# Layers 0 and 1 of a four-layer hybrid network: the convolution reads PSUM by image, the output projection runs among the steps of the scan, and the row update of layer 1 moves into layer 2

## The chip, the cores and the metric

One core of a Trainium2 chip runs the whole network once. The metric is the device time of that one launch in microseconds (us); less is better. Five engines work from queues of their own, each in order: TensorE (PE, matrix products and transposes into PSUM), VectorE (DVE), ScalarE (ACT), GpSimd (POOL), and SyncE (SP), which issues transfers. ACT and POOL issue transfers too.

## The reference

The input is four images of 256 channels by 1024 positions, in float32. What is computed, cut to what this change touches:

```python
# layer 0
u = layernorm(x)                                  # over the 256 channels of a position
zxbcdt = u @ in_w.T                               # z 256, xBC 512, dt 4
dt = softplus(dt + dt_bias)
xBC = silu(causal_depthwise_conv(xBC, conv_w, 4 taps) + conv_b)
for t in range(1024):                             # state: 4 heads of 64 x 128
    state = state * exp(-dt * exp(A_log)) + (dt * x_t) B_t;  y_t = state @ C_t
y = rms_normalise((y + Dp * x) * silu(z)) * rms_w
out = y @ out_w.T
att = sigmoid(relu(mean_over_positions(out) @ se1_w.T + se1_b) @ se2_w.T + se2_b)
x = x + out * att                                 # one att per image
# layer 1: theta, phi, g are products of x with one column each
y = theta * (sum_over_positions(phi * g) / 1024)  # per image
x = x + batchnorm(w_w * y + w_b) * bn_gamma + bn_beta   # statistics over all images
# layer 2: attention per image, then 8 experts, 2 for each row; layer 3: linear attention, then an LSTM of 1024 steps
```

## The kernel before

Positions lie on the 128 partitions: an image is 8 row tiles of 128 positions, the whole input is 32 row tiles. `s.rows` holds all 32 of them (256 floats a partition each) from layer 0 to the end of layer 2's attention. Float32 products appear in the profile as two PE instructions each, transposes as one.

**Projection** (`_project`, L215). Eight blocks of 512 positions. `load` fetches a block of x, turns it into rows (L241, L244) with the three columns of layer 1 beside it (L245), and normalises it (L133, L134 on DVE, L146, L147 on POOL, L153 on DVE). `turn` turns the normalised rows back (L162, L257), `project` makes z and dt (L270, L273, L274) and the four 128-channel chunks of xBC (L278), which ACT copies from PSUM to SBUF behind three columns of zeros (L281). After each second block `convolve` makes the four taps of a chunk: one on ACT (L288), three on DVE (L293), then silu on ACT (L296). PSUM has 2 slots for `p_x`, 4 for `p_w` and 2 for `p_z`.

**Decays** (`_decays`, L311). After the last block, once for all 32 tiles: softplus by Exp and Ln, then three products and Exp.

**Scan** (`_scan`, L356). Per tile of 128 positions: five products and transposes (L370, L371), the mask of decays (L381 on ACT, L383, L385, L386), the product inside the tile (L392), the state's share and the state's update (L401 to L409), then the gate (L412) and its squares (L414).

**Output** (`_out`, L417). Per image: 1/rms of 8 tiles (L426, L427 on POOL), diagonal matrices (L434) with which PE turns and scales the rows (L438, L442), their sum, the two small layers of the attention (L451 to L467), the weight times that attention (L469), six products with accumulation for the three columns of layer 1 (L473), and 8 products (L481) added to the rows (L484, L485). It is written after the scan of the next image; for the last image nothing follows it but layer 1.

**Layer 1** (`_layer1`, L488). A chain of small operations over all images (L505 to L549), `bn_beta` added to the rows on POOL (L552, 8 instructions) and 32 row updates on DVE (L554).

**Layer 2** (`_layer2_attention`, L575) loads its weights (L123), makes the product of the query and key weights (L602, L608), and then runs `front(b)` per image (`norm`, `turn`, `query`, `value`); the front of image b + 1 runs beside the scores of image b. After it `_lstm_constants` (L1281) loads and scales the LSTM's weights (L1286, L1289, L1290), and the plan of the experts follows (`_plan`, L957).

Outside blocks marked `manual_schedule` a planner orders the instructions of each engine: what is written first has the higher priority, but what is ready by its own estimates may go ahead. Tiles take their memory from pools; a tile waits until its slot is free.

Of the kernel before, what the change touches and what calls it, by code (L numbers as in the profile page):

```python
# [71 lines left out]
NW = {"w_l0": 260 + 512 + 256 + 64, "w_l2": 768 + 8, "w_l3": 768, "w_u": 768, "w_v": 768}  # L72
# [92 lines left out]
def _layer0_and_1(s):  # L165

    nc, tc = s.nc, s.tc
    off = DCONV - 1  # L170
    with ExitStack() as ctx:
        keep = ctx.enter_context(tc.tile_pool(name="l0_keep", bufs=1))
        w = keep.tile([P, C, NW["w_l0"]], F32, name="w_l0")
        nc.scalar.dma_start(w, s.d["w_l0"].rearrange("(k p) n -> p k n", p=P))
        se2 = keep.tile([NSE, D], F32, name="se2")
        nc.scalar.dma_start(se2, s.d["w_se2"])
        wide = keep.tile([P, 5, D], F32, name="wide")
        nc.scalar.dma_start(
            wide.rearrange("p i d -> p (i d)"), s.d["wide"].to_broadcast([P, 5 * D])
        )  # L180
        v = SimpleNamespace(
            w_zdt=w[:, :, :ZDT], w_xbc=w[:, :, ZDT : ZDT + 512], w_out=w[:, :, 772:1028],
            w_se1=w[:, :, 1028:1092], se2=se2, se2_b=wide[:, 0, :], beta=wide[:, 1, :],
            three=wide[:, 2:, :],
# [3 lines left out]
            xbc=[keep.tile([P, NXBC, off + L], F32, name=f"xbc{b}") for b in range(B)],  # L188
            zs=[keep.tile([P, TPI, D], F32, name=f"zs{b}") for b in range(B)],
            dtr=keep.tile([P, NT, NH], F32, name="dtr"),  # L190
            ss=keep.tile([P, NT], F32, name="ss"),
        )
        for x in v.xbc:
            nc.gpsimd.memset(x[:, :, :off], 0.0)
        for k in range(C):
            nc.vector.tensor_scalar_mul(
                v.w_out[:, k, :], v.w_out[:, k, :], s.col["rms_w"][:, k : k + 1]
            )
        _project(s, v)
        v.dt, v.decay, v.total, v.tail = _decays(s, keep, v.dtr)  # L200
        with ExitStack() as body:
            pools = SimpleNamespace(
                scan=body.enter_context(tc.tile_pool(name="ssm", bufs=2)),
                out=body.enter_context(tc.tile_pool(name="out", bufs=2)),
                ps=body.enter_context(tc.tile_pool(name="ssm_ps", bufs=2, space=PSUM)),
            )
            for b in range(B):
                _scan(s, v, pools, b)
                if b > 0:
                    _out(s, v, pools, b - 1)  # L210
            _out(s, v, pools, B - 1)
        _layer1(s, v)


def _project(s, v):  # L215
# [4 lines left out]
    with ExitStack() as ctx:  # L220
        one = ctx.enter_context(tc.tile_pool(name="proj_one", bufs=1))
        pool = ctx.enter_context(tc.tile_pool(name="proj", bufs=2))
        ps = ctx.enter_context(tc.tile_pool(name="proj_ps", bufs=3, space=PSUM))

        turner = one.tile([P, C, 3 + P], F32, name="turner")
        for k in range(C):
            nc.vector.tensor_copy(turner[:, k, 3:], s.ident)
            for j, name in enumerate(("theta_w", "phi_w", "g_w")):
                nc.vector.tensor_copy(turner[:, k, j : j + 1], s.col[name][:, k : k + 1])
        held = {}  # L230

        def load(i):
# [4 lines left out]
            for j in range(TPB):  # L237
                n = i * TPB + j
                p = ps.tile([P, C, 3 + P], F32, name="p_x", bufs=2)
# [6 lines left out]
            at = slice(i * TPB, (i + 1) * TPB)  # L246
            held[i] = _moments(s, pool, lambda j: s.rows[:, i * TPB + j, :], TPB)
            un = pool.tile([P, TPB, D], F32, name="un")
            _normalise(s, pool, un, s.rows[:, at, :], held[i])
            held[i] = un  # L250

        def turn(i):
            u = pool.tile([P, C, W], F32, name="u")
            for k in range(C):
                p = ps.tile([P, W], F32, name="p_w", bufs=4)
                _turn(s, p.rearrange("p (j t) -> p j t", t=P), held[i], k)
                nc.scalar.activation(  # L257
                    u[:, k, :], p, AF.Identity,
                    bias=s.col["norm_b"][:, k : k + 1], scale=s.col["norm_g"][:, k : k + 1],
                )  # L260
            held[i] = u

        def project(i):
            u = held.pop(i)
            b, t0 = divmod(i * W, L)
            for j in range(TPB):
                n = t0 // P + j
                p = ps.tile([P, ZDT], F32, name="p_z", bufs=2)
                for k in range(C):
                    nc.tensor.matmul(  # L270
                        p, u[:, k, bass.ts(j, P)], v.w_zdt[:, k, :], start=k == 0, stop=k == C - 1
                    )
                nc.scalar.activation(v.zs[b][:, n, :], p[:, :D], AF.Silu)  # L273
                nc.vector.tensor_add(v.dtr[:, b * TPI + n, :], p[:, D:], s.row["dt_bias"])  # L274
            for m in range(NXBC):
                p = ps.tile([P, W], F32, name="p_w", bufs=4)
                for k in range(C):
                    nc.tensor.matmul(  # L278
                        p, v.w_xbc[:, k, bass.ts(m, P)], u[:, k, :], start=k == 0, stop=k == C - 1
                    )  # L280
                nc.scalar.copy(v.xbc[b][:, m, off + t0 : off + t0 + W], p)  # L281

        def convolve(b):
            for m in range(NXBC):
                x = v.xbc[b][:, m, :]
                acc = pool.tile([P, L], F32, name="acc")
                tap = s.col["conv_w"][:, m * DCONV : (m + 1) * DCONV]
                nc.scalar.activation(  # L288
                    acc, x[:, off:], AF.Identity,
                    bias=s.col["conv_b"][:, m : m + 1], scale=tap[:, off:],  # L290
                )
                for j in range(off):
                    nc.vector.scalar_tensor_tensor(  # L293
# [281 lines left out]
def _layer2_attention(s):  # L575
# [10 lines left out]
    with ExitStack() as ctx:  # L586
# [222 lines left out]
        with tc.manual_schedule(engines=IN_ORDER):  # L809
# [13 lines left out]
            f.last()  # L823


def _layer2_experts(s):

# [838 lines left out]
```

## Time and profile before

| What | us |
|---|---|
| Median of 3 runs (3480.51 to 3481.63) | 3481.63 |
| The profiled execution, its own time | 3482.43 |
| Its span (first to last instruction) | 3480.7 |
| PE busy over the span | 3121.1 |
| DVE busy over the span | 1841.5 |
| ACT busy over the span | 1091.2 |
| POOL busy over the span | 534.8 |
| First scores of layer 2's attention (L739) start at | 386.25 |

Layers 0 and 1 and the first front of layer 2 are the first 386 us. The attention and the experts follow, and the LSTM takes more than half of the span. Busy time of PE is modelled, and its instructions overlap: a group's mean is longer than the distance from one to the next. Where the text uses that distance, it is the length of a run of equal instructions divided by their number.

### The profile page before, as it was taken

How to read it: one execution, taken by the hardware profiler on the slowest of the kernel's cores; microseconds unless marked ns; L12 is line 12 of the kernel's file. 1: busy time of each engine (PE TensorE's matmuls, PEld its weight loads, DVE VectorE, ACT ScalarE, POOL GpSimd, SP SyncE). 2: the span in 40 equal slices, each digit the busy share in tenths (PEclk: the TensorE clock that was granted, in tenths of full speed). 3: DMA queues.
4: the chain of work that ended last, by engine and by line, in shares of the span. 5: the costliest groups of instructions: out<-in, count | busy, mean ns of one | idle time of the engine just before them, and what ended most of it. 6: DMA issues, size and time to landing. Idle time of an engine off the chain costs nothing.

```text
span 3480.7 us, 143620 instructions
## 1 busy us (share of the span) xinstructions
PE 3121.1 (90%) x63578; PEld 2506.4 (72%) x63578; DVE 1841.5 (53%) x8172; ACT 1091.2 (31%) x4347; POOL 534.8 (15%) x752
## 2 busy tenths in 40 slices
PE   8797899969999979898998998998998998998887
PEld 5465567758888866777777777777777777777776
DVE  5686555541111133565655655655655665665555
ACT  5663222222222222233333332333332332332222
POOL 1153000024444420000100100100100100100000
PEclk9898899979999999999999999999999999999999
DMA  2000000046666640000000000000000000000000
GB/s 81 1 1 18 1 25 25 31 159 191 191 193 191 192 114 1 3 4 4 10 4 4 10 4 4 10 4 4 10 4 4 10 4 4 10 4 6 8 4 10
DMA packets 46003, 135.51 MB, mean 39 GB/s; under 512 B 4864, under 2 KB 34880, under 8 KB 40768
## 3 DMA queue, kind: packets, MB, share of 16 engines
q0 software_dynamic: 19008, 99.32, 9.4%
q1 hardware_dynamic: 24496, 21.27, 1.9%
q8 instruction: 499, 8.18, 1.0%
q10 hardware_dynamic: 1872, 5.68, 0.5%
q14 instruction: 128, 1.05, 0.1%
HBM read 103.95 MB, written 22.32 MB: 36 GB/s over the span
## 4 chain that ended last, share of the span: by engine, by line
PE 54%; DVE 26%; ACT 11%; issue 5%; POOL 1%; DMA 1%; ACTq 0%; DVEq 0%; POOLq 0%; SPq 0%
PE pre L1500 15%; DVE col L1511 11%; PE ph L1111 7%; PE po L1121 7%; PE pre L1462 6%; ACT tri L1514 5%; DVE scan L1523 5%; DVE hs L1534 4%; PE p_a L1420 3%; PE p_d L773 3%; PE p_s L739 3%; DVE acc L293 1%; PE p_o L481 1%; PE p_d L1214 1%; PE p_w L760 1%
## 5 line engine op out<-in xcount | busy, mean ns | idle before, releaser
L1500 PE MATMUL pre<-w_v,hs 128*4 128x64 f32 x49104 | 873.7, 219 | 211.5 <-DVE hs L1534 200.6
L1500 PEld LDWEIGHTS pre<-w_v,hs 128*4 128x4 f32 x49104 | 685.1, 86 | 399.1 <-DVE hs L1534 398.6
L1462 PE MATMUL pre<-xg,pick 128*128 128x64 f32 x6144 | 904.6, 283 | 0.0
L1462 PEld LDWEIGHTS pre<-xg,pick 128*128 128x128 f32 x6144 | 764.1, 191 | 117.9 <-issue 0.8
L1511 DVE STREAM_TRANSPOSE col<-pre 128x64 f32<-128x64 f32 x2048 | 484.9, 250 | 305.9 <-PE pre L1500 287.6
L1514 ACT ACTIVATE tri<-col 128x16 f32<-128x16 f32 x1024 | 229.3, 224 | 1182.4 <-DVE col L1511 1182.4
L1523 DVE TENSOR_TENSOR_SCAN scan<-tri 128x24 f32<-128x24 f32 x1024 | 216.4, 211 | 361.4 <-ACT tri L1514 361.4
L1428 POOL TENSOR_TENSOR xg<-xg,gate_bias 128x192 f32<-128x192 f32 x128 | 75.5, 590 | 1594.3 <-ACT xg L1427 1594.3
L1111 PE MATMUL ph<-xT,wt 128*128 128x256 f32 x1152 | 257.2, 381 | 0.4 <-ACT hT L1114 0.4
L1121 PE MATMUL po<-wt,hT 128*128 128x256 f32 x1152 | 254.6, 379 | 0.0
L1114 ACT ACTIVATE hT<-ph,wt 128x256 f32<-128x256 f32 x288 | 136.2, 473 | 369.6 <-PE ph L1111 359.8
L1111 PEld LDWEIGHTS ph<-xT,wt 128*128 128x128 f32 x1152 | 208.5, 190 | 43.2 <-ACT hT L1114 6.3
L1121 PEld LDWEIGHTS po<-wt,hT 128*128 128x128 f32 x1152 | 216.2, 190 | 28.0
L1532 DVE STREAM_TRANSPOSE gate<-row 128x64 f32<-128x64 f32 x1024 | 228.3, 223 | 0.6
L1521 ACT ACTIVATE row<-pre 128x64 f32<-128x64 f32 x1024 | 210.1, 205 | 0.5
L1539 DVE SCALAR_TENSOR_TENSOR tri<-hs,scan 128x8 f32<-128x8 f32 x1023 | 180.9, 177 | 36.2 <-DVE hs L1534 1.7
L1085 DVE COPY xT<-p_x 128x512 f32<-128x512 f32 x36 | 24.9, 692 | 228.7 <-PE p_x L1081 228.7
L1135 POOL DMA_INDIRECT acc<-y,rows x72 | 114.9, 1596 | 199.9 <-issue 89.1
L1133 DVE TENSOR_TENSOR y<-po,wt 128x256 f32<-128x256 f32 x72 | 30.6, 425 | 204.9 <-PE po L1121 204.9
L1420 PE MATMUL p_a<-w_u,u 128*32 128x192 f32 x1792 | 119.3, 338 | 0.0
L773 PE MATMUL p_d<-v,prT 128*128 128x256 f32 x512 | 117.6, 380 | 0.4 <-DVE v L658 0.4
L739 PE MATMUL p_s<-u,q 128*128 128x512 f32 x256 | 116.3, 596 | 0.0
(2376 smaller groups left out, 3250.4 us busy)
## 6 DMA issues: line engine op xcount, KB each, us to landing
xn<-xn SPq DMA_DIRECT2D x8, 516.0 KB, 3.5
x<-in_x_dram SPq DMA_DIRECT2D x16, 256.0 KB, 3.2
rows<-acc SPq DMA_DIRECT2D x8, 512.0 KB, 7.2
out_dram<-part SPq DMA_DIRECT2D x64, 64.0 KB, 1.7
acc<-rows SPq DMA_DIRECT2D x7, 512.0 KB, 2.9
r<-xn,rows POOLq DMA_INDIRECT x72
acc<-y,rows POOLq DMA_INDIRECT x72
w_l<-in_w_l_dram ACTq DMA_DIRECT2D x1, 1092.0 KB, 9.6
```

The lines of the kernel that those rows point to most:

```text
L739: nc.tensor.matmul(p[:, h, :], v.q[:, k, bass.ts(j, P)], v.u[:, k, bass.ts(h, W)], start=k == 0, stop=k == C - 1,)
L773: nc.tensor.matmul(p, prT[:, n, :], images[g // TPI].v[:, n, :], start=n == 0, stop=n == TPI - 1)
L1111: nc.tensor.matmul(ph, w1[:, k, bass.ts(m, P)], xT[:, k, :], start=k == 0, stop=k == C - 1)
L1121: nc.tensor.matmul(po, hT[:, m, bass.ts(j, P)], w2[:, m, :], start=m == 0, stop=m == NHC - 1,)
L1420: nc.tensor.matmul(p[32 * j : 32 * (j + 1), :], u3[i * SG // P][:, k, bass.ts(i % (P // SG), 32)], w_u[:, k, j * Q : (j + 1) * Q], start=k ...
L1462: nc.tensor.matmul(p, pick[:, r].rearrange("p j r -> p (j r)"), xg[i][:, v], start=True, stop=t == 0,)
L1500: nc.tensor.matmul(p[32 * j : 32 * j + B, :], hs[:, t - 1, k * B : (k + 1) * B], w_v[:, k, j * Q + v.start : j * Q + v.stop], start=False, ...
L1511: nc.vector.transpose(col[:, g * C : (g + 1) * C, :].rearrange("p n r -> p (n r)"), pre[t % 2][g])
L1514: nc.scalar.activation(z[:, 2:50].rearrange("p (g q) -> p g q", g=2)[:, :, ::3].rearrange("p g (k b) -> p (g k) b", k=C), col[:, :, :B], A ...
L1521: nc.scalar.activation(row, pre[t % 2][2], AF.Tanh)
L1523: nc.vector.tensor_tensor_scan(scan, z[:, 0 : 3 * S], z[:, 26 : 26 + 3 * S], 0.0, ALU.mult, ALU.add)
L1532: nc.vector.transpose(gate.rearrange("p n r -> p (n r)"), row)
```

## The change

- **Start.** The weights of layer 0 come in two parts (`w_in`, 772 columns, and `w_o`); the fold of `rms_w` into `w_out` is written later (after image 1) and takes a factor 0.5. The identity part of `turner` is copied by POOL. `bn_beta` is added to the rows in `load`.
- **Convolution by image.** `u` of a whole image is kept; `chunk(b, m)` makes 128 channels by 1024 positions in a PSUM tile of two banks (`p_c`, 2 slots), and ACT and DVE read it there. The copy to SBUF and the zeros are gone. `turn` and `gates` share `p_z` (2 slots).
- **Decays in two parts.** Image 0 within the projection, images 1 to 3 after tile 3 of the scan.
- **Output among the scan's steps.** A list `aside` of pieces (`_turned` for two tiles, `_attended` for an image, `_product` for a tile); after each tile of the scan up to two are taken. The columns of layer 1 come from a transposed weight instead of six accumulating products.
- **Last output and layer 1** in `_last`, in written order, with products of layer 2's weights and filling products (`busy`) between. The weights of layer 2 are loaded after the projection.
- **Row updates** of layer 1 are made in `norm` of layer 2; for the first block `norm` works in two halves.
- `_lstm_constants` is written behind the second expert tile; the `weights` pool has one slot.

```diff
@@ _layer0_and_1 @@
+        with tc.tile_pool(name="w_in", bufs=1, side="right") as pool:
+            w = pool.tile([P, C, NIN], F32, name="w_in")
+            nc.scalar.dma_start(w, s.d["w_l0"][:, :NIN].rearrange("(k p) n -> p k n", p=P))
+            nc.scalar.dma_start(v.beta, s.d["bn_beta"].to_broadcast([P, D]))
...
+            nc.scalar.dma_start(w, s.d["w_l0"][:, NIN:].rearrange("(k p) n -> p k n", p=P))
+            nc.scalar.dma_start(v.se2, s.d["w_se2"])
...
+        nc.scalar.dma_start(s.w_l2, s.d["w_l2"].rearrange("(k p) n -> p k n", p=P))
@@ _project @@
+            nc.gpsimd.tensor_add(mine, mine, _bc(v.beta, 1, TPB))
...
+        def chunk(b, m):
+            p = ps.tile([P, L], F32, name="p_c")
...
+            acc = v.acc.tile([P, L], F32, name="acc", bufs=2)
+            nc.scalar.activation(
+                acc, p, AF.Identity, bias=s.col["conv_b"][:, m : m + 1], scale=tap[:, off:]
+            )
+            for j in range(off):
+                late = off - j
+                nc.vector.scalar_tensor_tensor(
+                    acc[:, late:], p[:, : L - late], tap[:, j : j + 1], acc[:, late:],
+                    ALU.mult, ALU.add,
                 )
+            nc.scalar.activation(v.xbc[b][:, m, :], acc, AF.Silu)
...
+        for b in range(B):
+            i = b * BPI
+            for j in range(BPI):
+                gates(i + j)
+                if b + 1 < B:
+                    load(i + BPI + j)
+            if b == 0:
+                nc.scalar.activation(v.na, s.row["A_log"], AF.Exp)
+                _decays(s, v, pool, lambda: ps.tile([P, W], F32, name="p_z"), 0, TPI)
+            for m in range(NXBC):
+                chunk(b, m)
+                if b + 1 < B and m < BPI:
+                    turn(i + BPI + m)
@@ _scan @@
+        for c in range(TPI):
+            _scan_tile(s, v, pools, b, c, state)
+            if b == 0 and c == 3:
+                _decays(s, v, pools.scan, lambda: _small(pools, P, W), TPI, NT)
+            for _ in range(2):
+                if aside:
+                    aside.pop(0)()
+            if c % 2 and b * TPI + c < NT - 1:
+                aside.append(
+                    lambda b=b, c=c, yT=yT, part=part: _turned(s, v, pools, b, c - 1, yT, part)
+                )
...
+    with tc.manual_schedule(engines=IN_ORDER):
+        _last(s, v, pools, yT, part)
+def _turned(s, v, pools, b, c, yT, part, between=None):
...
+    rstd = pool.tile([P, 2], F32, name="rstd", bufs=3)
+    nc.gpsimd.tensor_tensor(rstd, rstd, s.power[:, :2], ALU.pow)
...
+    for k in range(C):
+        for j in range(2):
+            nc.tensor.matmul(
+                p[:, k, bass.ts(j, P)], v.zs[b][:, c + j, bass.ts(k, P)], diag[:, j, :],
+                start=True, stop=True,
             )
+        nc.scalar.activation(
+            yT[:, k, c * P : (c + 2) * P], p[:, k, :], AF.Identity,
+            accum_out=part[:, k, c // 2 : c // 2 + 1],
+        )
@@ _attended @@
+    a3 = pool.tile([P, C, 3], F32, name="a3")
+    nc.vector.scalar_tensor_tensor(a3, _bc(att_c, 2, 3), 1.0, v.three, ALU.add, ALU.mult)
+    p = _small(pools, P, 3 * C)
...
+                p[:, bass.ts(m, 3)], v.w_outT[:, k, bass.ts(m, P)], a3[:, k, :],
...
+    nc.vector.scalar_tensor_tensor(
+        w[:, :, :D], _bc(att, 1, C), 1.0, v.w_out, ALU.add, ALU.mult
+    )
@@ _last @@
+    def busy(n):
+        p = bank("pd")
+        for i in range(n):
+            nc.tensor.matmul(p[:, :P], s.lower, s.upper, start=True, stop=True)
...
+    for c in range(TPI):
+        for k in range(C):
+            nc.tensor.matmul(
+                p[:, c, :], yT[:, k, bass.ts(c, P)], w[:, k, D:], start=k == 0, stop=k == C - 1
+            )
...
+    made = list(product(2))
...
+    nc.vector.tensor_copy(s.l1_row, p)
+    busy(16)
@@ _layer2_attention @@
+            def norm(i, parts=1):
...
+                        nc.vector.scalar_tensor_tensor(
+                            mine[:, j, :], s.l1_row, s.l1_y[:, m : m + 1], mine[:, j, :],
+                            ALU.mult, ALU.add,
+                        )
@@ _expert_tiles @@
+            if beside and i == first + 1:
+                beside()
```

## The prediction

> **What bounds the kernel now.** First the page's busy tenths in 40 slices of 87 us. The change touches the first four and a half and the ninth; there the clock that PE was granted is not full:
>
> ```profile
> PE   8797899969999979898998998998998998998887
> PEclk9898899979999999999999999999999999999999
> ```
>
> Then busy time by engine, cut where the chain of work changes hands:
>
> ```profile
> 0.00:12.05 12.05, 2.11 (x8) 1.81 (x8) 2.19 (x23) 2.03 (x3) 1.90 (x15) 1.00 0.83 295
> 12.05:126.80 114.75, 107.22 (x435) 69.92 (x436) 76.36 (x196) 76.88 (x135) 10.09 (x16) 1.00 0.09 31
> 126.80:149.30 22.50, 3.61 (x12) 2.01 (x10) 17.33 (x22) 13.19 (x18) 0.00 (x0) 0.62 0.00 0
> 149.30:302.50 153.20, 140.06 (x782) 106.73 (x781) 126.49 (x311) 96.02 (x299) 80.14 (x106) 0.95 0.00 1
> 302.50:349.90 47.40, 29.57 (x134) 22.35 (x134) 21.55 (x76) 7.46 (x31) 13.42 (x18) 0.79 0.10 34
> 349.90:362.60 12.70, 5.12 (x16) 3.89 (x16) 12.70 (x33) 0.74 (x2) 0.00 (x0) 0.63 0.00 0
> 362.60:386.25 23.65, 18.84 (x64) 11.90 (x65) 15.97 (x60) 3.92 (x6) 5.03 (x8) 0.82 0.00 0
> ```
>
> The columns are length, then busy time of PE, its weight loads, DVE, ACT, POOL, then PE's clock. I call the rows A to G and all that follows H. PE bounds B and nearly D. C, E, F and half of G are chains in which PE stands: its clock falls to 0.62 to 0.82. A mean over all 386 us would hide this.
>
> The chain of waits tells what the tails are made of:
>
> ```profile
> 127.28 4.88 DVE acc L293 x4
> 142.12 1.28 ACT L344
> 309.71 9.35 PE p_o L481 x32
> 330.09 9.38 PE p_o L481 x32
> 340.14 2.31 DVE all L505
> 349.87 12.76 DVE rows L554 x32
> 724.81 0.88 DVE w_v L1290
> ```
>
> In C the last image's taps run alone on DVE, then the decays with three table loads. In E two images' outputs run after one another, then layer 1. F is row updates only. The last line is a piece of the LSTM's constants on the chain between attention and experts.
>
> Groups that price the pieces (min/median/max in ns where three numbers stand):
>
> ```profile
> L293 DVE SCALAR_TENSOR_TENSOR acc<-xbc,cols,acc x48: 1253/1280/1286, 45.1 to 139.6; 128x1024 f32<-128x1024 f32 x48
> L408 DVE TENSOR_TENSOR state<-state,total x24: 407/496/2355, 159.9 to 298.6; 128x256 f32<-128x256 f32 x24
> L403 DVE TENSOR_TENSOR y_in<-pst,head x28: 406/414/426, 159.6 to 301.2; 128x256 f32<-128x256 f32 x28
> L552 POOL TENSOR_TENSOR rows<-rows,wide 128x1024 f32<-128x1024 f32 x4 | 9.4, 2354 | 6.7 <-DVE rows L484 6.7
> ```
>
> A DVE operation with two SBUF inputs (state) stretches up to 2355 ns, the length of the POOL addition beside it; one that reads PSUM (y_in) never passes 426.
>
> **The change part by part.** The sum is made against the profiled execution's own 3482.4 us (span 3480.7), 0.8 above the median of 3481.6.
>
> *A, start.* PE begins at 7.43 and stalls until 12.05, because DVE waits until 11.31 for the whole weight transfer to scale `w_out` (L196) with the first copies queued behind it. That fold moves to image 1. But ACT, in order, issues one transfer more (six for five) before its first copy; its fourth and fifth issues came 2.3 and 2.8 us after the one before. Between nothing gained and 4 us: I take -2, since the ACT issues are the nearer limit.
>
> *B, projection.* Demand of PE, from distances inside runs: chunks 128 instructions x 0.43 = 55.0, gates 128 x 0.22 = 28.2, rows 128 x 0.11 = 14.4, turns 64 x 0.11 = 7.0; 104.6 us, unchanged but for 4 transposes. 16 acc operations of ACT now read PSUM; 32 ACT copies of 0.58 (18.7 us) and the zeros go, but ACT had 38 us to spare, so I count nothing for them. POOL gets 8 x 2.35 = 18.8 us of additions; conv reads PSUM, so by L403 it is not stretched; the additions stand before later rstd on POOL's queue, at most 2.35 each time, beside chunk products. A tap from PSUM is not in the trace: L403 and L396 with one PSUM input took what SBUF pairs took (414 against L404's 414), so I add zero; bounds -1 to +4 for 48. Image 0's decays: at least four more table loads than the three of C, 4 x 1.28 = 5.1 us of ACT, cover is PE's first two chunks; I take 2 on the path (0 to 5), booked in C. New limit: two p_c slots. A slot is held 3.44 (PE) + 1.24 + 3 x 1.25 + 0.45 of hops = 8.9, so one chunk per 4.45 against 3.44 of PE. PE fills the gap with turns and next gates if the planner places them. From 104.6 (all filled) to 122 (4 x 30.2: 17.8 chunks + 7.0 + 3.6 + 1.8). I take 112, nearest to the old 114.75, since the mutual waiting stays: -2.8.
>
> The Trainium skill, "VectorE: DVE Perf Modes", section "Rules for kernel authors", speaks against this: with many operations on a matmul's output, copy PSUM to SBUF first; its errata section gives 62 more cycles of start for a PSUM source. By that, an estimate from its 0.96 GHz, 48 taps cost 3.1 us more DVE; the rows above show 0, and DVE had 38 us to spare in B.
>
> *C, tail.* After the last chunk: 1.24 + 3 x 1.25 + 1.06 + hops = 6.4, plus up to 3.75 of the chunk before and the 2 from above. Decays of images 1 to 3 sit in the scan. 22.5 becomes 9 (6.4 to 13.4): -13.5.
>
> The Trainium skill, "ScalarE: Activation LUTs", "What ACT_TABLE_LOAD costs", puts a load at about 2.7 us and asks to group functions by set, against splitting the decays. The page's price makes four loads 10.8 us; the trace has 1.283 each.
>
> The load of layer 2's weights (776 KB, one issue of 0.45 on ACT's queue, formerly at 342.5) now waits for the memory of `w_in` and `acc`; what ACT has queued behind it, the first tiles' masks and copies, cannot pass the last silu. That is inside the 9; its data are wanted in E only, 150 us later, so its landing costs nothing.
>
> *D, scan.* The first 16 tiles had almost no output beside them: zs (L412) from 159.25 to 212.21, 15 intervals, 3.53 each. Image 3, with a whole output beside it, took 302.1 - 258.0 = 44.1, 5.5 per tile. Output work of PE per image: turning 32 x 0.125 = 4.0, products 7.4, attention 3.5 (new small products included), 15. D held about 33 of this, now three whole images and three quarters of a turning: 48, so +15. Gone from D: 12 junk operations beside each image's weight (0.35 to 0.84 each) and four POOL additions which stretched state by 1.5 to 1.9 each. New: DVE's decays 3.5, two table loads 2.6, POOL's rstd for pairs (15 x 0.92 for 3 x 1.85). With 5.1 per tile for images 1 to 3 (44.1 less about 3 an image): 9.9 to the first zs + 7 x 3.53 + 3 of turning + 24 x 5.1 = 160; I take 158. If everything packs as the first tiles do, 145; with the old 5.5 and table loads on the path, 172. +4.8.
>
> *E, last output and layer 1.* One image's outputs leave entirely (20.4, from 309.71 to 330.09). The rest, from the rows: squares 0.7, rstd 1.1, diag 0.6, turn and yT twice 2.6, pooled to weight columns 4.5 without junk, fillers 1, thirty-two 3-column products 4.2, sum 0.3: 15. Layer 1 took 349.8 - 342.5 = 7.3; products in its way add 3.5. About 26 (20 to 32): -21.4. The fillers delay any late chain by at most their own 0.9; they sit where PE waits.
>
> *F.* 32 updates of 0.40 leave: -12.7. 24 of them run beside layer 2's scores, where PE is busy 25.0 of each 25 us and DVE 11 to 15; without that cover +9.6.
>
> *G.* 8 updates (3.2) enter image 0's norms; half-norms start the second rstd earlier, weights and the key product (L602) are already made, and PE enters warm. I take 25 (21.5 to 28.5): +1.4.
>
> *H.* L1289 and L1290 stood on the chain with 2.1 us between 721 and 726: -2. Their two issues (0.37 each on ACT), four copies on ACT and POOL's one fill now stand between the experts' operations, on queues less than half full there; the transfers (1.5 MB) run beside the experts' weights, where the DMA share is 0.2 to 0.8: -4 to +3.
>
> Sum: -2 - 2.8 - 13.5 + 4.8 - 21.4 - 12.7 + 1.4 - 2 = -48.2, so 3434.2; from the median 3433.4. I say 3434.
>
> **The rivals.**
> 1. *PSUM becomes the bound of the projection.* For it: 8.9 us per slot, and gates now share p_z with turns and wait for dtr on DVE behind 1.28 us taps (PE already waited 6.1 for dtr). Against: B's PE had 7.5 idle only. B 122 and C 13: +14, 3448.
> 2. *The planner does not place the pieces as written*, the change does half of what it says. For it: before, products of image 0 came 16 us after its pooled sum. Then D is 172 and a few products remain for E (+7): 3455.
> 3. *Slower: pieces block the in-order queues.* A turned piece is a chain over POOL, DVE, PE, ACT, PE, ACT of 3.6 us, 15 of them; three attentions of 5.5; 24 products with add and copy of 1.5. Wholly exposed 107 us on top of 119 for bare tiles (9.9 + 31 x 3.53): D 226, 3502. It decides from D above 206, when 87 of the 107 are exposed. Against: before, image 3 hid more than half.
> 4. *Row updates or constants find no cover in H*: +9.6 and +5, 3449; against it stands DVE's idle half.
>
> **How the numbers follow.** Likeliest case 0.69; rival 1 0.11, rival 2 0.10, rival 4 0.03, slower 0.05, no visible change 0.02. The ends of the terms (A 2, B 9, C 3.5, D 13.5, E 6, G and H 3.5 each to a side), taken as independent, make 18: the likeliest case's own range is 3416 to 3452. The wider range reaches over rivals 1, 2 and 4: 3412 to 3464. Faster by over 0.2% (7 us, about what a measurement of this kernel tells from no change): 0.93; same 0.02; slower 0.05. All bad ends together make -3 us, so only rival 3 is slower.
>
> **What would show it.** First scores (L739) near 340 instead of 386.25. Squares of tile 0 before 140 and of tile 31 near 290. One run of 8 products, no second, after the last square; no run of 32 row updates; no DVE operation beside POOL's additions above 1.3 us in B. If zs intervals of images 1 to 3 exceed 6.5 us, or chunks come 4.4 us apart with PE idle between, I am wrong in D or B. If the first scores come at 340 and the time does not fall by 40, the loss lies in H.

## The result, and the profile after

The changed kernel takes 3492.2 us (3488.7 to 3494.5, 7 runs) where the kernel before took 3481.6 in the same runs: a ratio of 1.0031, interval 1.0019 to 1.0043. It is 10.6 us slower; 48 us faster was predicted.

The profiled execution of the changed kernel has a span of 3487.0 and was the shortest of the seven (3488.74), so the two traces show 6.3 us of the 10.6. What the other six executions did longer was not traced; under no_fillers stands a trace of the same orders in which a lower clock of PE in the projection and the scan costs such an amount.

The same cuts in both traces, by the first operation that belongs to the next stage (first zs and last zs are DVE's zs multiplications, L412 before and L461 after; "row" is the copy of layer 1's row, L549 and L695; "scores" the first p_s, L739 and L870):

| stage | before | after | moved | predicted |
|---|---|---|---|---|
| start to first zs (A, B, C) | 159.2 | 161.9 | +2.7 | -18.3 |
| first to last zs (D) | 142.9 | 163.2 | +20.3 | +4.8 |
| last zs to row (E) | 47.3 | 38.9 | -8.4 | -21.4 |
| row to first scores (F, G) | 36.8 | 24.9 | -11.9 | -11.3 |
| first scores to the end (H) | 3094.5 | 3098.1 | +3.6 | -2 |

D and E before, in the columns explained below:

```profile
159.20:302.10 142.90, 132.02 (x750) 100.84 (x748) 123.31 (x304) 88.08 (x277) 76.63 (x100) 0.98 0.00 1
302.10:349.40 47.30, 29.57 (x134) 22.35 (x134) 21.48 (x74) 7.86 (x32) 13.42 (x18) 0.80 0.10 34
```

Busy time of PE, its weight loads, DVE, ACT and POOL in these stages of the changed kernel, then PE's granted clock, the DMA share and GB/s (the first row ends where PE resumes after its stall at the start):

```profile
0.00:13.72 13.72, 2.43 (x9) 1.88 (x9) 2.10 (x22) 2.02 (x4) 2.21 (x13) 1.00 0.81 280
13.72:161.90 148.18, 124.25 (x490) 79.14 (x491) 101.31 (x233) 88.62 (x147) 33.67 (x32) 0.94 0.08 24
161.90:325.10 163.20, 144.51 (x861) 115.53 (x860) 121.40 (x303) 99.66 (x336) 72.38 (x118) 1.00 0.00 1
325.10:364.00 38.90, 34.08 (x140) 31.02 (x141) 8.26 (x32) 2.75 (x10) 3.13 (x14) 0.61 0.07 21
364.00:388.90 24.90, 20.54 (x89) 13.45 (x89) 20.75 (x69) 3.92 (x6) 5.36 (x9) 0.93 0.00 1
```

In the scan PE is busy 144.5 of 163.2, before 132.0 of 142.9; in the last output it is busy 34 of 39, yet at a clock of 0.61. Over D and E together PE was busy 161.6 us before and 178.6 after: the new arrangement gives PE more to do (the key product moved here, three-column products, fillers), and the low clock in E stretches it. The trace of before has PE at a clock of 0.50 from 221.1 to 227.9, the changed one nowhere in its scan, so at an equal clock the scan would have lost more than 20.3.

The start. DVE in order of time:

```profile
12.97 0.62 DVE L305 TENSOR_SCALAR w_o<-w_o,cols 128x256 f32<-128x256 f32 x2 [6.05 <-DMA w_o<-in_w_l_dram]
13.51 0.15 DVE L249 COPY of_x<-p_x 128x6 f32<-128x6 f32 x1
```

The planner has put the scaling of the output weights, written beside image 1, back ahead of the first copy; it waits for a transfer that is now issued later.

Image 0's decays and first convolutions on ACT, in order of time:

```profile
38.85 1.28 ACT L354 ACT_TABLE_LOAD   x1
40.14 0.23 ACT L354 ACTIVATE e<-e 128x32 f32<-128x32 f32 x1
40.28 1.19 ACT L290 ACTIVATE acc<-p_c,cols 128x1024 f32<-128x1024 f32 x1
41.48 1.28 ACT L356 ACT_TABLE_LOAD   x1
...
52.67 1.28 ACT L368 ACT_TABLE_LOAD   x1
...
54.27 1.28 ACT L299 ACT_TABLE_LOAD   x1
55.56 1.06 ACT L299 ACTIVATE xbc<-acc 128x1024 f32<-128x1024 f32 x1
56.64 1.28 ACT L368 ACT_TABLE_LOAD   x1
```

The planner interleaves decays and convolution one by one, with a table load at nearly each change, seven between 38 and 66. PE's longest waits from 12 to 150, with how often and the longest:

```profile
PE p_c L284 <- DVE dt L363: 6.8, 1, 6.8
PE p_x L245 <- DVE of_x L249: 5.9, 1, 5.9
PE p_c L284 <- DVE acc L295: 4.5, 4, 2.0
```

The 6.8 end at 50.37, and they are DVE's: from 44 to 52 DVE is busy 8.00 of 8.00 us, ACT with its loads 2.33. DVE has the taps of two chunks and the decays mixed in its queue, and one of the decays' operations, of only 32 columns and with two SBUF inputs, takes 2.22 us beside POOL's addition of beta. The first two lines are the changed kernel's, the last is that of no_beta, which leaves the additions out:

```profile
42.57 2.37 POOL L254 TENSOR_TENSOR rows<-rows,beta 128x1024 f32<-128x1024 f32 x1 [1.56 <-DVE e L355]
42.77 2.22 DVE L359 SCALAR_TENSOR_TENSOR den<-e,none 128x32 f32<-128x32 f32 x1
42.74 0.19 DVE L358 SCALAR_TENSOR_TENSOR den<-e,none 128x32 f32<-128x32 f32 x1
```

The last output, PE in order of time (a turning, the three-column products, the products):

```profile
327.57 0.71 PE L481 MATMUL p_o<-diag,zs 128*128 128x128 f32 x4 [3.48 <-DVE diag L477]
...
338.95 1.92 PE L605 MATMUL pd<-upper,lower 128*128 128x128 f32 x8
340.65 1.71 PE L539 MATMUL p_o<-a,w_outT 128*128 128x3 f32 x8
342.22 1.20 PE L605 MATMUL pd<-upper,lower 128*128 128x128 f32 x4
343.21 6.83 PE L624 MATMUL ptr<-w_att,yT 128*128 128x3 f32 x32
349.90 3.76 PE L634 MATMUL pst<-w_att,yT 128*128 128x256 f32 x8
```

After 3.5 us without work the granted clock was 0.50 in every 2 us from 330 to 358, though PE was busy nearly throughout.

### The profile page after: what moved, and what is told of

Read it like the earlier page. It is cut to its first block, busy times and chain, and to the rows that moved or that the text cites. A ratio compares the mean times of both kernels' runs of the same rounds, so it can differ in the third digit from the quotient of the medians.

```text
span 3487.0 us, 143953 instructions
## 1 busy us (share of the span) xinstructions
PE 3143.3 (90%) x63722; PEld 2531.1 (73%) x63722; DVE 1831.8 (53%) x8135; ACT 1089.8 (31%) x4359; POOL 542.8 (16%) x776
## 4 chain that ended last, share of the span: by engine, by line
PE 27%; DVE 20%; ACT 10%; issue 5%; DMA 1%; ACTq 0%; POOL 0%; DVEq 0%; POOLq 0%
PE pre L1633 15%; DVE col L1644 11%; PE pre L1595 6%; ACT tri L1647 5%; DVE scan L1656 5%; DVE hs L1667 4%; PE p_a L1553 3%; PE p_d L1347 1%; DMA acc<-y,rows 1%; PE p_k L1315 1%; ACTq L1647 0%; PE p_d L1379 0%; PE p_d L1355 0%; PE p_w L1335 0%; PE p_w L163 0%
## 5 line engine op out<-in xcount | busy, mean ns | idle before, releaser
L1216 DVE COPY xT<-p_x 128x512 f32<-128x512 f32 x36 | 24.9, 692 | 228.4 <-PE p_x L1212 228.4
L870 PE MATMUL p_s<-u,q 128*128 128x512 f32 x256 | 116.4, 596 | 0.0
```

## The experiments

Each time is beside the kernel before in runs on the same chip. "Against the changed kernel" is the distance to before less 10.6. Each interval reaches 3 to 6 us to a side, so distances of fold_on_pool, no_beta, rstd_early, tile_later and no_fillers are not clear of noise by the times alone, nor is combined2 apart from combined; there the stages in the traces carry the reading.

| run | us | before | ratio (interval) | against the changed kernel |
|---|---|---|---|---|
| decays_once | 3477.5 | 3481.7 | 0.9987 (0.9977 to 0.9996) | -14.8 |
| old_projection | 3481.0 | 3481.7 | 1.0000 (0.9990 to 1.0009) | -11.3 |
| two_taps | 3475.0 | 3478.9 | 0.9986 (0.9976 to 0.9995) | -14.6 |
| fold_on_pool | 3486.2 | 3479.8 | 1.0017 (1.0007 to 1.0027) | -4.2 |
| no_beta | 3488.5 | 3479.8 | 1.0022 (1.0012 to 1.0031) | -1.9 |
| output_after_image | 3480.0 | 3481.7 | 0.9997 (0.9988 to 1.0007) | -12.4 |
| rstd_early | 3490.5 | 3480.0 | 1.0025 (1.0014 to 1.0035) | -0.1 |
| tile_later | 3485.6 | 3478.9 | 1.0016 (1.0006 to 1.0025) | -3.9 |
| no_fillers | 3487.7 | 3480.0 | 1.0020 (1.0010 to 1.0029) | -3.0 |
| wide_fillers | 3483.8 | 3480.0 | 1.0005 (0.9996 to 1.0015) | -6.9 |
| rows_moved | 3476.6 | 3481.7 | 0.9985 (0.9975 to 0.9994) | (on before) -5.1 |
| both | 3464.4 | 3480.0 | 0.9949 (0.9932 to 0.9966) | -26.3 |
| combined | 3459.4 | 3479.8 | 0.9942 (0.9925 to 0.9958) | -31.0 |
| combined2 | 3457.3 | 3479.8 | 0.9933 (0.9917 to 0.9950) | -33.1 |

### The projection

**decays_once**

```diff
-            if b == 0:
-                nc.scalar.activation(v.na, s.row["A_log"], AF.Exp)
-                _decays(s, v, pool, ..., 0, TPI)
...
+        nc.scalar.activation(v.na, s.row["A_log"], AF.Exp)
+        _decays(s, v, pool, ..., 0, NT)
...
-            if b == 0 and c == 3:
-                _decays(s, v, pools.scan, ..., TPI, NT)
```

> The changed kernel with the decays of all four images computed once, after the last convolution, instead of image 0's inside the projection and the others inside the scan. Theory 1 (the table loads and DVE operations of image 0's decays cost the projection its start): PE's stall of 6.75 us before the second product goes, the first acc of a convolution starts near 37 instead of 40.3, the last silu of a convolution near 141 instead of 152.5; then decays of about 9 us stand alone, first zs near 160 instead of 161.9, and the scan loses about 3 us of decays: 3486 to 3489. Theory 2 (two PSUM slots of 4.4 us bind the projection whatever the decays do): the last silu stays above 148, the decays come on top: first zs 167 to 171, 3495 to 3501.

First acc 39.6, last silu 144.6, first zs 156.3 (161.9 with the split). Theory 1 held in kind and was too small: from first to last zs it is 158.1 instead of 163.2 as well, since the scan no longer carries the decays of three images. Table loads of this kernel for the decays up to the first zs: three among image 3's chunks (122.95 to 128.00), three about the last silu (141.67 to 145.62), none beside image 0. So the planner did not leave the one set bare behind the projection either, and still it costs less than two sets, of which the first stands among image 0's taps.

**old_projection**: the functions of before for the projection, fed with the changed kernel's loads, then one set of decays.

```diff
-            chunk(b, m)
+            project(i)
+            if i % BPI == BPI - 1:
+                convolve(i // BPI)
```

> The changed kernel with the projection of the kernel before (half images, copies to SBUF, taps from SBUF) and one set of decays after it; the additions of beta stay in load, scan, outputs, layer 1 and layer 2 stay as changed. Theory 1 (the projection part gained nothing, since its own gain was eaten by slots and decays): first zs at 158 to 162, 3486 to 3492. Theory 2 (convolution from PSUM did bring what it was to bring and the loss lies in the scan and the last output alone): first zs 168 or later and 3498 to 3505. Theory 3 (projection part is the loss): first zs by 150, 3475 to 3480.

First zs 162.1, as theory 1 had it, but the time is under its range: as in decays_once the scan without decays is shorter (161.6). Against decays_once, which differs in the layout of the projection only (whole images and taps from PSUM against half images, copies and taps from SBUF, with other PSUM slots), the new layout comes out 5.8 us ahead at the first zs (156.3 against 162.1). By the times it is 3.5, with intervals that just overlap. So that part of the change reads as a gain; what was put around it ate it.

**two_taps**

```diff
-            for j in range(off):
+            for j in range(1, off):
```

> The changed kernel with two of the three taps on DVE; the first tap is left out of the computation. A slot of PSUM is then held 1.25 us less. Theory 1 (two slots bind the projection, each held 8.6 us): the last image's chunks come 3.6 to 3.8 apart instead of 4.3, the last silu falls from 152.5 to 145 or earlier, first zs at 152 to 156, 3483 to 3487. Theory 2 (the slots bind only the last image, where no turns and gates are left to fill PE): last silu 148 to 151, first zs 158 to 160.5, 3488 to 3491.

The kernel leaves one of the taps out. Last silu 142.7, first zs 151.1, 10.8 us earlier than with three taps, for 16 x 1.27 = 20 us less work on an engine that was busy 101 of the 148 us. Theory 1 holds: the acc of the last image's four chunks start at 127.4, 130.9, 135.8 and 138.6, 3.7 apart on average, where the changed kernel has 132.2, 135.7, 141.3 and 145.1, 4.3 apart. The edit takes work from DVE as well as holding time from the slots, so the two are not told apart. The time, 3475.0, lies below the range of both theories: the trace has 1.6 us less from last zs to row and 2.9 behind the first scores as well, and 3.3 more in the scan, where PE's clock was 0.50 from 196.8 to 203.6. PE's waits in it:

```profile
PE p_c L284 <- DVE num L361: 4.2, 1, 4.2
...
PE p_c L284 <- DVE acc L295: 1.2, 2, 0.7
```

The wait for acc falls from 4.5 to 1.2 and the one in image 0's decays from 6.8 to 4.2: whatever stands with the taps in DVE's queue while a PSUM slot is held reaches PE.

**fold_on_pool**

```diff
-                nc.vector.tensor_scalar(
+                nc.gpsimd.tensor_scalar(
                     v.w_out[:, k, :], v.w_out[:, k, :], s.col["rms_w"][:, k : k + 1], 0.5,
```

> The changed kernel with one line on another engine: the scaling of the output weights by rms_w, which stands in DVE's queue ahead of the first copies and waits there for its transfer until 12.97, is done by POOL. Theory 1 (the stall at the start costs what it lasts): DVE's first of_x copy at about 9.7 instead of 13.51, PE's idle time of 5.88 us shrinks to about 2, first zs and all later times come 2 to 4 us earlier: 3488 to 3490. Theory 2 (the projection has slack and takes the start back): first acc within 1 us of 40.3, 3491 to 3494.

The one line moves, and DVE starts when ACT has made the first rows:

```profile
9.58 0.17 DVE L249 COPY of_x<-p_x 128x6 f32<-128x6 f32 x1 [2.50 <-ACT rows L248]
...
13.32 0.94 POOL L305 TENSOR_SCALAR w_o<-w_o,cols 128x256 f32<-128x256 f32 x2 [10.45 <-DMA w_o<-in_w_l_dram]
```

PE resumes at 9.80 instead of 13.72, first zs comes at 158.7 instead of 161.9. Theory 1: the projection gave back 0.7 of 3.9.

**no_beta**

```diff
-            nc.gpsimd.tensor_add(mine, mine, _bc(v.beta, 1, TPB))
```

> The changed kernel without POOL's eight additions of beta beside the projection; the addition of beta is left out of the computation. Theory 1, that of the prediction (they stretch nothing that is on the path): first zs and time as in the changed kernel, 3490 to 3494. Theory 2 (the additions stretch DVE operations on two SBUF inputs and delay POOL's rstd, which un and so PE wait for): first zs 3 to 8 us earlier, 3484 to 3489.

First zs 160.0, 1.9 earlier: between the theories. The cause is the row above: `den`, 2.22 us beside the addition, takes 0.19 without it, and PE's wait in image 0's decays falls from 6.8 to 4.7. So the additions cost about 2 us at the first zs, not zero, by the stretch that theory 2 names. The 1.9 in the times are within their noise.

### The scan and the outputs

**output_after_image**

```diff
-            for _ in range(2):
-                if aside:
-                    aside.pop(0)()
...
+        for f in done:      # the pieces of image b-1, after image b's tiles
+            f()
```

> The changed kernel with the pieces of an image's output written all together after the next image's scan, as before, instead of two pieces after each tile; the pieces themselves, the last output and layer 1 stay. Theory 1 (pieces written among the tiles block the in-order queues): first to last zs falls from 163 to 145-152, the row of layer 1 comes 20 us later after the last zs (39 + 20), the time is 3495 to 3502. Theory 2 (PE, DVE and ACT have the same work and the written order does not set the pace): first to last zs stays at 160 to 164 with images 1 to 3 at 42 to 44 each and what follows the last zs grows by 0 to 15: 3492 to 3507.

First to last zs fell to 138.6, 24.6 less and below theory 1's range, and what follows the last zs grew by 13.7 only (52.6), below its price: net 10.9. The time, 3480.0, is below both theories' ranges. Images 1 and 2 take 28.9 and 36.7 from last zs to last zs instead of 44.5 and 44.3; image 3, beside which a whole output remains, 42.8. PE's waits from first to last zs, first in this kernel, then in the changed one:

```profile
PE pst L455 <- POOL xw L447: 3.3, 2, 2.6
PE pd L432 <- ACT m_h L434: 2.2, 1, 2.2
```

```profile
PE p_o L481 <- DVE diag L477: 7.2, 8, 1.1
PE pst L455 <- POOL xw L447: 4.8, 5, 1.2
PE pd L432 <- ACT m_h L434: 2.2, 1, 2.2
```

PE idles 7 us in the one (131.5 busy of 138.6) and 19 in the other. So 13 of the 24.6 us are PE work moved behind the last zs, and the other 11.6 are idle time that is gone. With the pieces written last the planner uses them to fill; that a tile's own work waited behind them when they were written among the tiles is the reading of this, and the next two runs ask at which wait.

**rstd_early and tile_later** ask whether it is the visible wait, DVE for rstd and PE for diag behind it.

```diff
+                r = _root(s, v, pools, b * TPI + c - 1)    # rstd_early
```
```diff
-                if aside:
+                if aside and aside[0][0] < b * TPI + c:    # tile_later
```

> The changed kernel with POOL's two operations for a pair's rstd written right after the pair's second tile, before the next tile, and the rest of the piece after that next tile as now. Theory 1 (in the scan DVE stands 7 us for rstd and PE 6 for the diag behind it, and with a pair every second tile that sets the pace of 5.5 us per tile): both waits under 1.5 us, first to last zs 150 to 158 instead of 163: 3480 to 3488. Theory 2 (it is the amount of written-in work in the queues, this wait is only where it shows): the waits move to py, pst or p_o, first to last zs stays 160 to 164: 3489 to 3494.

> The changed kernel with each turning written one tile later than now, when its pair's squares are long done; nothing else. Theory 1 (in the scan the pieces cost by standing in DVE's and PE's queues ahead of a tile's work, waiting for a rstd that comes late): DVE's wait for rstd falls from 7.2 to under 2 and PE's for diag from 6.1 to under 2, first to last zs from 163.2 to 152 to 158: 3482 to 3489. Theory 2 (the amount of PE, DVE and ACT work written into a tile sets its 5.5 us, wherever in it): first to last zs within 3 us of 163, 3489 to 3495.

rstd_early left both waits where they were (PE's 6.1, DVE's 7.7 from 162 to 300; 6.1 and 7.2 in the changed kernel). DVE and ACT have the same order as there, and on POOL three of the 15 first operations of a pair moved by one place: the planner undid the edit, and it tells nothing. tile_later did change the order. PE's wait for diag halves, and others take its place:

```profile
PE pst L456 <- POOL xw L448: 5.3, 6, 1.3
PE p_o L482 <- DVE diag L478: 3.4, 4, 1.6
PE pd L433 <- ACT m_h L435: 2.2, 1, 2.2
PE p_o L367 <- DVE a L364: 1.7, 1, 1.7
```

First to last zs is 162.7, as theory 2 has it. But this execution had PE at 0.50 in two stretches of the scan (173.2 to 176.6 and 193.7 to 197.1), and the profiled one of the changed kernel had none. Three other traces with the changed kernel's order on DVE and ACT had two such stretches too and took 166.5 (no_fillers, no_beta) and 166.2 (rstd_early); two without any took 163.1 (wide_fillers) and 163.3 (fold_on_pool). The scans of no_fillers and of tile_later, and one stretch:

```profile
165.20:331.70 166.50, 147.30 (x857) 117.61 (x856) 121.38 (x304) 99.70 (x336) 72.29 (x118) 0.98 0.00 1
164.60:327.30 162.70, 147.92 (x860) 116.97 (x859) 121.70 (x303) 98.50 (x336) 72.27 (x118) 0.98 0.00 1
173.20:176.60 3.40, 3.40 (x13) 3.06 (x12) 2.08 (x5) 2.11 (x7) 1.53 (x3) 0.50 0.00 0
```

Like against like, tile_later's scan is 3.5 to 3.8 us shorter, PE idles 14.8 us instead of 19.2, and its time is 3.9 better. So writing the turnings one tile later is worth some 4 us, more than theory 2 had and less than theory 1. Theory 1's own sign, DVE's wait for rstd under 2, did not come (7.5 in the whole scan, 9.1 in the changed kernel), so which wait carries the rest stays open.

**both**: decays_once and output_after_image in one kernel.

> The decays of all images once after the projection, and each image's output written after the next image's scan, in one kernel; the rest as changed. Theory 1 (the two losses lie in different stages and add): first zs near 156, last zs near 295, first scores near 367, 3463 to 3468. Theory 2 (what one gives the other loses, as both remove the same slow tiles): 3474 to 3480.

First zs 156.5, last zs 288.9, first scores 369.6: theory 1, the two losses add (14.8 and 12.4 alone, 26.3 together). The scan takes 132.4 with PE busy 128.5.

### The last output

**no_fillers and wide_fillers**

```diff
     def busy(n):
-        p = bank("pd")
-        for i in range(n):
-            nc.tensor.matmul(p[:, :P], s.lower, s.upper, start=True, stop=True)
+        pass                                               # no_fillers
```
```diff
-            nc.tensor.matmul(p[:, :P], s.lower, s.upper, start=True, stop=True)
+            nc.tensor.matmul(p, s.lower, s.w_l2[:, 0, :W], start=True, stop=True)
...
-    _turned(..., lambda: (w0(), busy(2)))
+    _turned(..., lambda: (w0(), busy(6)))                  # wide_fillers
...                                                         # one or two at each later place, 6 for 16 at the end
```

> The changed kernel without the 128-column fillers on PE in the last output (they compute nothing that is used). Theory 1 (fillers stand in PE's in-order queue on the chain and do not bring the clock back): 39.3 us from the last zs to the row of layer 1 become 33 to 36, the granted clock is 0.50 there as with them, image 0's front in layer 2 loses up to 2: 3487 to 3490. Theory 2 (fillers do what they stand there for): the clock stays at 0.50 longer, the stage takes 40 to 44: 3493 to 3498.

> The changed kernel with the fillers made 512 columns wide, six of them ahead of the last turning, one or two at each later place. Theory 1 (the clock follows columns streamed, and narrow products with a 128-column weight load each count as little): no row at 0.50 between the last zs and the pooled sum's products, the 32 three-column products take 3.4 to 5 instead of 6.83, the stage from last zs to row is 29 to 34 instead of 39.3: 3482 to 3488. Theory 2 (the clock falls for the wait before the turning whatever PE does, or fillers cost as much as the clock gives): stage 38 to 45, 3491 to 3499.

Without fillers the stage is 33.8 us instead of 38.9, at the same clock of 0.50, so the narrow fillers only stood in the way. In this trace first and last zs came later (165.2, 331.7), though DVE, ACT and POOL run the same operations in the same order up to there: PE's clock was at 0.50 for 23.9 us ahead of the first zs instead of 17.1, and for 6.8 us instead of none in the scan, and each of these two stages is 3.3 us longer. So that is not the edit's. It is also the nearest reading of the 2.9 to 5.8 us by which six executions of the changed kernel were longer than the profiled one, though none of the six was traced. With wide fillers it is 31.7, in theory 1's range. PE in order of time:

```profile
324.44 4.51 PE L605 MATMUL pd<-w_l,lower 128*128 128x512 f32 x10
328.79 0.61 PE L481 MATMUL p_o<-diag,zs 128*128 128x128 f32 x4
...
340.29 1.96 PE L605 MATMUL pd<-w_l,lower 128*128 128x512 f32 x4
342.09 3.63 PE L624 MATMUL ptr<-w_att,yT 128*128 128x3 f32 x32
345.58 3.66 PE L634 MATMUL pst<-w_att,yT 128*128 128x256 f32 x8
```

The clock is 1.00 in every 3 us from 300 to 345, and the same 32 products take 3.63 instead of 6.83. It is 1.00 until 345.5, the end of those narrow products, and 0.50 from 345.75 to 349, with no gap ahead of it. That the fall follows from the narrow width is the nearest reading; bridging the gap ahead of the turning and widening the fillers were not tried apart.

### The row updates alone

**rows_moved**: the kernel before with layer 1's updates in layer 2's norms, nothing else.

```diff
-        for n in range(NT):
-            nc.vector.scalar_tensor_tensor(
-                s.rows[:, n, :], row, y[:, n : n + 1], s.rows[:, n, :], ALU.mult, ALU.add
-            )
...
+                        nc.vector.scalar_tensor_tensor(
+                            mine[:, j, :], s.l1_row, s.l1_y[:, m : m + 1], mine[:, j, :], ...
```

> The kernel before with only one thing changed: the 32 row updates of layer 1 moved into layer 2's norms, image 0's first norm in two halves. Theory 1 (updates find cover in attention): 12.7 us go from the chain, 3.2 come back in image 0's front, 0 to 3.4 in attention: 3472 to 3476. Theory 2 (the 3.4 us which attention took longer in the changed kernel are the price, and image 0's front gets slower too): 3477 to 3481. Rival (no cover, DVE late in each step): 3481 to 3485.

The time, 3476.6, lies at the join of theories 1 and 2. Row to first scores is 26.2 instead of 36.8, so 10.6 of the 12.7 is gained; from first to last scores it takes 309.3, as in the changed kernel, where before took 305.9. The place is the first scores. DVE there:

```profile
379.35 2.46 DVE L626 SCALAR_TENSOR_TENSOR rows<-l_row,l_y,rows 128x256 f32<-128x256 f32 x6
381.72 1.22 DVE L749 TENSOR_REDUCE top<-p_s 128x1 f32<-128x1024 f32 x1
```

The first maximum starts 7.2 us after the first scores (3.7 before). The six updates shown, for later rows, stand ahead of it for 2.4 us; others stand between the additions of the values just before. DVE's idle time in the scores behind was there, but the planner did not wait for it.

### Together

**combined** is both, with wide_fillers and fold_on_pool; **combined2** writes the last image's first three turnings ahead of the products of the image before.

```diff
-    for f in done:
+    for f in before[:5] + done + before[5:]:               # combined2
         f()
```

> Decays once after the projection, each image's output written after the next image's scan, 512-column fillers in the last output, the scaling of the output weights on POOL. If the gains add (14.7 and 12.2 together gave 27.8; wide fillers 8.4; the start 2 to 4): 3450 to 3455. If the fillers give less where the stage is ordered otherwise: 3456 to 3462.

> As the combined kernel, with the last image's first three turnings written ahead of the products of the image before. Theory 1 (24 turning products then run where PE waits in the attention's chain of image 2, instead of 3.7 to 5.5 us after its products): 3 to 5 us below the combined kernel. Theory 2 (the turnings' copies on ACT push the chain back by as much): within 2 us of it.

combined gained 4.7 us over both, less than the sum of the parts alone (6.9 and 4.2). combined2 is 2.1 below it by the medians, at the edge between its theories and within the noise; in the traces its first scores come 5.5 us earlier (358.7 against 364.2), but combined's profiled execution was the slowest of its four, so not all of that is the edit's. The stages of combined2, cut as above:

```profile
9.80:153.00 143.20, 123.81 (x486) 79.69 (x486) 99.64 (x230) 85.28 (x146) 34.75 (x34) 0.94 0.10 33
153.00:284.10 131.10, 127.17 (x760) 101.50 (x760) 108.81 (x276) 89.08 (x296) 75.14 (x115) 1.00 0.00 1
284.10:333.90 49.80, 47.07 (x245) 35.47 (x244) 14.70 (x55) 9.46 (x42) 4.90 (x17) 0.97 0.05 17
333.90:358.70 24.80, 21.98 (x68) 11.97 (x67) 20.74 (x69) 3.92 (x6) 5.35 (x9) 0.93 0.00 0
```

PE is busy 174 of the 181 us from first zs to row (second and third line), at nearly full clock. It is faster than both kernels: 22.5 us under before, ratio 0.9933 (0.9917 to 0.9950).

## Why the prediction was wrong

- **A, start** (-2; +1.7): the step "that fold moves to image 1" failed. It did not move; the planner placed it by the data it needs and not where it was written. The bound "between nothing gained and 4 us" left out a loss. fold_on_pool shows the price, 3.2 us at the first zs.
- **B and C, projection and tail** (-16.3; +1.0): three terms. "Image 0's decays: I take 2 on the path" was at least 5.6 (decays_once), since decays and taps were dealt out in turns on DVE and the wait reached PE. Of table loads there are 14 up to the first scores, before 5, where the forecast had "at least four more". "I take 112, nearest to the old" for two PSUM slots was rival 1's ground: the chunks of image 3 came 4.3 apart (rival 1 had 4.45), and a tap less brings 10.8. The additions of beta, booked at nothing, cost 2: no tap was stretched, as forecast, but the decays that moved beside them have an operation with two SBUF inputs, 2.22 us where the sign to look for was "above 1.3". The mechanism itself was right, 5.8 us over the old layout. Rival 1 named a true cause; its +14 lacked the decays, the start and beta.
- The taps' price held: 1.27 to 1.28 us from PSUM, 1.28 from SBUF. The 62 cycles more that the Trainium skill, "VectorE: DVE Perf Modes", errata section, has for a PSUM source are not seen in these rows. The second rule weighed, to group functions by table set (the Trainium skill, "ScalarE: Activation LUTs", "Rules for kernel authors"), points the way decays_once went: seven loads stand between 38 and 66, and with the decays done once none does. But the trace does not show that the loads were the price: PE's 6.8 us end at DVE, and DVE was the busy engine there. That page's "What ACT_TABLE_LOAD costs" splits its 2.66 us for a switch into 1283 ns of load and about 1380 of drain; the trace's loads are 1.28 too, and the next operation starts 0.01 us behind one (38.85 and 1.28, then 40.14), so the drain is not seen here.
- **D, scan** (to 158 from the decays' end, some 148 from first to last zs; 163.2): the step "5.1 per tile for images 1 to 3" failed, 5.5 stayed, 10 us in all. The decays of images 1 to 3, named as 3.5 and 2.6 but in none of the sum's four terms, cost 3.3 in image 0's tiles (31.0 us between its first and last zs, 27.7 in decays_once, which is the sum's 24.7 and 3). What taking junk operations and POOL's additions out of the scan was to bring did not show. Written behind the tiles instead, the pieces leave D at 138.6 with 13.7 more behind it (output_after_image), so it is rival 3's mechanism, pieces ahead in in-order queues, at 173 in its count (163.2 and the 9.9 to the first zs), well short of the 206 from which it decided alone. Several losses together made the kernel slower, and for all bad ends together I had "-3 us": the ends themselves were set too near.
- **E** (26; 38.9): two terms. "Thirty-two 3-column products 4.2" were 6.83, and "the fillers delay any late chain by at most their own 0.9" was 5 (no_fillers). The first is the granted clock of 0.50, on which E's terms did not reckon; at full clock the products take 3.63 and the stage 31.7.
- Two slips that change nothing: B's 122 is 4 x 30.2 = 120.8, and of the four POOL additions in before's scan three stretched `state`, not four.
- D and E by PE's own work: 148 and 26 make 174 us, and PE's busy time in the best arrangement found is 174 of 181. The forecast thus took PE to have no idle time at all; its work over these stages was never summed.
- **F and G** (-11.3; -11.9) held. **H** (-2; +3.6): the constants left the stretch from last scores to the experts' first products unchanged (61.8 before, 61.9 after), and the updates' cover failed at the first scores, 3.4 (rows_moved; 309.3 or 309.4 us from first to last scores in every kernel with the moved updates, 305.9 before). The 3.6 as a whole is less sure: behind the first scores, traces of the changed kernel and of kernels that keep its code there lie between 3092.1 and 3098.8. Rival 4 named that place at 9.6.

## What to carry to other kernels

Where a planner orders the queues, moving a line in the program moves a priority: small background pieces belong behind the work they are to fill, and a part is only "off the chain" if something forbids the planner to pull it in front. Before booking stages as shorter, sum the work of the engine that is left, at the clock that it will be granted. Small operations that share a queue with the taps of a held PSUM slot were dearer here split up than done once, late. And before two traces are compared by a stage, compare PE's granted clock in it: here 3 us of a stage came and went with it while the order of the work was the same.

## What the runs showed of the hardware

- PE counted as busy 2.0 of 2.0 us in each 2 us from 336 to 350 at a granted clock of 0.50 all the while, in narrow products and 128-column fillers; with 512-column fillers the clock stayed at 1.00 in that part of the stage and the same products took about half.
- The clock fell at the end of 32 three-column products without any idle time ahead of them (1.00 until 345.5, 0.50 from 345.75 to 349 in wide_fillers).
- With the changed kernel's order on DVE and ACT, traces differ by stretches of about 3.4 us at a clock of 0.50 in the scan: none in the changed kernel, wide_fillers and fold_on_pool (163.2, 163.1, 163.3 us), two in no_fillers, no_beta and rstd_early (166.5, 166.5, 166.2), so some 1.6 us for each, an estimate from these six.
- A DVE operation of 32 columns with two SBUF inputs took 2.22 us beside a POOL addition of 2.37, and 0.19 without it; the taps, with one input in PSUM, never passed 1.28 us beside such additions.
